# Weight products in three float32r passes, and a projected attention vector spread through DRAM, in a gated graph network kernel

## The chip, the cores and the metric

The kernel runs on one core of a Trainium2 chip. The metric is the device time of one execution in microseconds. The five engines are named as in the profile: PE is the matrix engine (PEld are its weight loads), DVE the vector engine, ACT the scalar engine, POOL the general engine, and SP the queue that issues most DMAs.

## The reference

There are 64 independent graphs of 256 nodes with 256 features each (all float32), and a 0/1 adjacency matrix of 256 x 256 for each. Two layers are applied.

```python
def layer_0(h, adj, weight, w_ih, w_hh, b_ih, b_hh):
    A = (adj != 0)
    for i in range(3):
        m = h @ weight[i]
        aggr = A.T @ m                       # per graph
        h = gru_cell(aggr, h, w_ih, w_hh, b_ih, b_hh)
    return h

def gru_cell(inp, h, ...):
    i_r, i_z, i_n = split(inp @ w_ih.T + b_ih)
    h_r, h_z, h_n = split(h @ w_hh.T + b_hh)
    r, z = sigmoid(i_r + h_r), sigmoid(i_z + h_z)
    n = tanh(i_n + r * h_n)
    return (1 - z) * n + z * h

def layer_1(x, adj, W, a):                   # graph attention
    h = x @ W.T
    e = leaky_relu((h @ a_left)[:, :, None] + (h @ a_right)[:, None, :])
    alpha = softmax(where(adj == 0, -1e9, e))
    return alpha @ h

x = x + layer_0(relu(layernorm(x)), adj, ...)
x = x + layer_1(relu(layernorm(x)), adj, W, a)
```

## The kernel before

The graphs are worked in 32 pairs. A pair of graphs gives 512 columns[...]. States are kept transposed (features on the partitions), in two blocks of 128 features.

**Setup.** The matrices that don't depend on the graphs are formed once. Since `A.T @ (h @ weight[i]) @ w_ih.T` equals `(A.T @ h) @ (weight[i] @ w_ih.T)`, the kernel forms the product G of `weight[i]` and `w_ih.T` for each of the three steps (L436 to L450). The weights come by DMA (`w load`, L363), are turned on PE by transposes (L374 and L420) and copied to SBUF by ACT (L381). A product block is 128 x 384. There are 12 of them: three steps, two halves of 768 columns, and two blocks of rows. Each takes two float32 matmuls (L446), which the trace shows as four records.

**Factors.** The large matmuls of the gates run in float32r. To keep float32 accuracy, `factor` (L392) makes three parts of each matrix: part 0 on ACT (L395), part 1 on DVE (L397) and part "d" on DVE (L400). `split` (L469) makes three such parts of each operand that comes from the graphs, on ACT (L472) and DVE (L473, L475). A gate's product (`gate`, L487) is then formed in three steps: the parts 0 and 1 ("top", L497), a scaling of the bank by ACT (L511), and the part d on top of it ("rest", L502).

**The attention vector.** The scores need `h @ a_left`, which is `x @ (W.T a_left)`. The kernel forms the two rows `W.T a` (L459 to L467). It broadcasts each column of `a` to 128 columns, so that one matmul gives the row on all 128 partitions, and copies the bank of 128 x 512 to `va` on DVE. The "dot" operations on DVE (L715) read `va`.

**The gates.** Each of three steps of a pair has `prop` (L618: the sum over neighbours), then for each of two feature blocks the gates r, nh (hidden part of n), ni (input part of n) and z. ACT does tanh for r (L637), n (L647) and z (L650), and DVE combines them (L642, L645, L654, L656, L658). `back` turns the state for the next step on PE (L685), or by DMA (L522, L527) with a copy on ACT (L535).

**Attention.** Normalisation (L550 to L563), dots (L715), leaky (L741), mask and max (L744, L746) and exp (L752) are followed by `mix` (L769), `project` (L778, or L792 for the last pairs, in float32), and the result (L797). The right-hand scores of all pairs but the last go through a row in DRAM and are spread to 128 partitions by a second DMA (L724, L727). The last pair is worked in finer pieces: its third step of gates in two halves of 256 columns ("of 0" and "of 1"), and its attention for each block of 128 rows (L807 to L838).

**What sets the order.** Nothing is issued in program order. Every operation is recorded with a duration, a latency and the buffers that it reads and writes, and a planner (`Plan.run`, L139) places them all. It takes the operation that can start first by its own estimates, and among those that can start together the one with the lowest priority value:

```python
                    if fits and (best is None or (t, o.prio, o.seq) < best[0]):
                        best = ((t, o.prio, o.seq), o)
```

The priority value comes from due times and from the latencies of what follows. A table `LEAD` (L27) shifts the priority of operations by name. Names of the first pair begin with "first", those of the last two pairs with "late" and "last"; an entry without such a word works on all pairs. The result is one fixed sequence for each engine.

Of the kernel before, what the change touches and what calls it, by code (L numbers as in the profile page):

```python
# [10 lines left out]
F32 = mybir.dt.float32  # L11
# [3 lines left out]
AF = mybir.ActivationFunctionType  # L15
ALU = mybir.AluOpType
# [8 lines left out]


LEAD = {  # L27
    "w load": 17000, "w d": -3000, "in 0 eps": -2000, "in 0 relu": 71000, "in 1 stats": -3000, "in 1 relu": 57000,
    "h0 0": 3000, "prop 0": 4000, "g0 0": -24000, "g0 1": -19000, "prop 1": 30000, "g1 1": 23000, "r 0 topT": 2000,
    "ni 0 topF": -18000, "u add 0": 1000, "z 0 topF": -114000, "z 0 rest": 11000, "z 0": 55000, "d add 0": -14000,  # L30
    "r 1 topT": -55000, "nh 1 rest": 5000, "ni 1 topF": -23000, "z 1 topF": -162000, "z 1 scale": -94000,
    "z 1": 51000, "d sub 1": -3000, "d add 1": -14000, "back copy 1": -43000, "mask 0": -6000,
    "mid 1 stats": -52000, "max 1": -19000, "c0 0": 12000, "late h0 d": -6000, "late prop 0": 13000,
    "late g0 0": -52000, "late r 0 topT": -7000, "late nh 0 topF": -29000, "late r 1 topT": -8000,
    "late ni 1 topF": -30000, "late tanh 1": -20000, "last A": 11000, "last in 0 stats": 9000,
    "last in 0 eps": 1000, "last prop 1": 19000, "last g1 0": 12000, "last r 0 topT": -5000,
    "last r 0 rest": -45000, "last nh 1 rest": -3000, "last lo 0": -88000, "last back 1": -80000,
    "last ni 0 of 0 topF": 18000, "last nh 1 of 0 rest": -5000, "last ni 1 of 0 topF": 19000,
    "last r 0 of 1 topF": -19000, "last nh 0 of 1 topF": -34000, "last ni 0 of 1 topF": -37000,
}  # L40


# [164 lines left out]
def tile_gated_gnn_then_gat(  # L207
# [39 lines left out]
    nc = tc.nc  # L247
    P = 128
    B, N, D = x.shape
    L = weight.shape[0]  # L250
    NB = N // P
    DB = D // P
    G = 2
    E3 = 3 * D
# [6 lines left out]
    const = ctx.enter_context(tc.tile_pool(name="const", bufs=1))  # L261
    psum = ctx.enter_context(tc.tile_pool(name="psum", bufs=1, space=bass.MemoryType.PSUM))
    plan = Plan(WINDOW, LEAD)
# [7 lines left out]
    dram = ctx.enter_context(tc.tile_pool(name="dram", bufs=1, space=bass.MemoryType.DRAM))  # L271
    plan.slot_class("line", [dram.tile([1, N], F32, name=f"line{i}") for i in range(4)])

    ALL = (0, 1)
    ONE = (0,)

    def parts(b):
        return b.t[:, :GN].rearrange("p (k d) -> p k d", k=2)
# [3 lines left out]
    def pe(name, n, fn, **kw):  # L282
        return plan.op(name, "PE", n, n + 220, fn, **kw)

    def act(name, n, fn, **kw):
        plan.op(name, "ACT", n, n + 170, fn, **kw)

    def dve(name, n, fn, **kw):
        plan.op(name, "DVE", n, n + 160, fn, **kw)

    def dve2(name, n, fn, **kw):
        plan.op(name, "DVE", n, n + 160, fn, port=True, **kw)
# [8 lines left out]
    MM, TR, PROP, PASS = 432, 109, 120, 232  # L301
    A512, V512, S512, VP256, C512 = 475, 605, 660, 392, 522
    LINE, SPREAD = 4600, 4600
    SPLIT = 4096.0
    C = 1.0 / SPLIT
    BELOW = 1.0 - C / 2
# [4 lines left out]
    vec = const.tile([P, 2 * DB + 2 * EB], F32, name="vec")  # L311
# [8 lines left out]
    va = const.tile([P, 2, D], F32, name="va")  # L320
# [15 lines left out]
    def setup():  # L336
# [6 lines left out]
        def load_rows():  # L343
# [7 lines left out]
           r=[(rw, ONE), ("ident", ONE)], w=[(pt, ONE)])  # L351
# [5 lines left out]
        def rows_of(src, nblk):  # L357

            view = src.rearrange("(b q) d -> q b d", q=P)
            res = []  # L360
            for r0 in range(0, nblk, 2):
                b = Buf("full")
                dma("w load", 256, lambda b=b, r0=r0: nc.sync.dma_start(parts(b), view[:, r0 : r0 + 2, :]), w=[(b, ONE)])  # L363
                res += [(b, 0), (b, 1)]
            return res

        def transposed(dst, region, blocks, whole=None):

            def go_for(c):
                pt = Buf("bank")  # L370

                def go():
                    for r, (b, k) in enumerate(blocks):
                        nc.tensor.transpose(pt.t[:, ts(r, P)], parts(b)[:, k, ts(c, P)], ident)  # L374

                n = len(blocks)
                pe("w turn", TR * n, go, r=[(b, ONE) for b, _ in blocks] + [("ident", ONE)], w=[(pt, ONE)])
                w = n * P if whole is None else whole

                def copies():  # L380
                    nc.scalar.copy(dst(c)[:, :w], pt.t[:, :w])  # L381
                    if w < n * P:
                        nc.scalar.mul(dst(c)[:, w:], pt.t[:, w : n * P], 0.5)

                act("w copy", (140 if w == n * P else 260) + n * 110, copies, r=[(pt, ONE)], w=[region(c)])

            for c in range(DB):
                go_for(c)

        H = E3 // 2  # L390

        def factor(m, b, n, dst, key, bank=True):  # L392

            src = lambda: b.t[:, :n]
            act("w 0", (100 if bank else 140) + 0.75 * n, lambda: nc.scalar.activation(dst(0), src(), AF.Copy, scale=C * BELOW),  # L395
                r=[(b, ONE)], w=[(f"fac{m}", (key + (0,),))])
            (dve if bank else dve2)("w 1", 75 + 1.04 * n, lambda: nc.vector.scalar_tensor_tensor(  # L397
                dst(1), dst(0).bitcast(F32), -SPLIT, src(), op0=ALU.mult, op1=ALU.add),
                r=[(b, ONE)], w=[(f"fac{m}", (key + (0,),))])
            dve2("w d", 75 + 1.04 * n, lambda: nc.vector.tensor_sub(dst(2), dst(1).bitcast(F32), dst(0).bitcast(F32)),  # L400
                r=[(f"fac{m}", (key + (0,),))], w=[(f"fac{m}", (key + (1,),))])

        def part_of(m, kb, half):
            return lambda j: fac[m][:, j, kb, ts(half, H)]

        def halves():
            return [[Buf("full") for _ in range(2)] for _ in range(DB)]

        def whole(T, blocks, n=E3):
            for half in range(2):  # L410
                transposed(lambda c, half=half: T[c][half].t[:, :H], lambda c, half=half: (T[c][half], ONE),
                           blocks[3 * half : 3 * half + 3], min(max(n - half * H, 0), H))

        def bank_of(blocks, c):

            pt = Buf("bank")

            def go():
                for r, (b, k) in enumerate(blocks):
                    nc.tensor.transpose(pt.t[:, ts(r, P)], parts(b)[:, k, ts(c, P)], ident)  # L420

            pe("w turn", TR * len(blocks), go, r=[(b, ONE) for b, _ in blocks] + [("ident", ONE)], w=[(pt, ONE)])
            return pt
# [7 lines left out]
        for kb in range(DB):  # L431
            factor("hh", whhT[kb], H, part_of("hh", kb, 1), (kb, 1), bank=False)
        wih_n = rows_of(w_ih, EB)
        wihT = halves()
        whole(wihT, wih_n)
        for i in range(L):  # L436
            w_n = rows_of(weight[i], DB)
            w_T = Buf("full")
            transposed(lambda c, w_T=w_T: parts(w_T)[:, c, :], lambda c, w_T=w_T: (w_T, (c,)), w_n)
            for half in range(2):  # L440
                for db in range(DB):
                    pg = Buf("bank")

                    def go(pg=pg, half=half, db=db, w_T=w_T):
                        for kb in range(DB):
                            nc.tensor.matmul(pg.t[:, :H], parts(w_T)[:, kb, ts(db, P)], wihT[kb][half].t[:, :H],  # L446
                                             start=(kb == 0), stop=(kb == DB - 1))

                    pe("G", 3 * MM, go, r=[(w_T, ALL)] + [(wihT[kb][half], ONE) for kb in range(DB)], w=[(pg, ONE)])
                    factor(i, pg, H, part_of(i, db, half), (db, half))  # L450
        W_n = rows_of(W, DB)
        Wb = W_n[0][0]
        for c in range(DB):
            w_T = bank_of(W_n, c)
            dve("w keep", 330, lambda c=c, b=w_T: nc.vector.tensor_copy(wT[:, c, :], b.t[:, :D]), r=[(w_T, ONE)], w=[("wT", (c,))])
            factor("W", w_T, D, lambda j, c=c: fac["W"][:, j, c, :], (c,))
        pl = Buf("bank")

        def go():  # L459
            for n in range(2):  # L460
                for ob in range(DB):
                    c = n * DB + ob
                    nc.tensor.matmul(pl.t[:, ts(n, D)], vec[:, c : c + 1].to_broadcast([P, P]), parts(Wb)[:, ob, :],
                                     start=(ob == 0), stop=(ob == DB - 1))

        pe("va", 4 * MM, go, r=[(Wb, ONE), ("vec", ONE)], w=[(pl, ONE)])
        dve("va copy", V512, lambda: nc.vector.tensor_copy(va, pl.t.rearrange("p (n d) -> p n d", n=2)), r=[(pl, ONE)], w=[("va", ONE)])  # L467

    def split(name, v, bank=False):  # L469

# [369 lines left out]

    TOPS, SLOT = {}, 20
    setup()
    for p in range(NPAIR):
        if p > 0:
# [31 lines left out]
```

## Time and profile before

| | |
|---|---|
| three runs | 2074.25, 2075.97 and 2076.62 us |
| span of the profiled execution | 2066.4 us |
| PE busy | 2045.3 us (99%) |
| DVE busy | 1737.0 us (84%) |
| ACT busy | 1761.8 us (85%) |
| L446, products G | 48 records of 128 x 384 |
| L497 and L502, gates | 2328 + 2328 and 1164 + 1164 matmuls |

A row of the profile's groups names the line, the engine, the operation and what it writes and reads. After a bar stand the total busy time and the mean time of one, and after a second bar the engine's idle time just before such instructions, with what ended it. The chain that ended last is followed back from the last instruction, at each step to what released it. Matmul ends are modelled and overlap the next start, so the time of a matmul is best read from the chain or from one start to the next.

### The profile page before, as it was taken

Reading aid. Unit: us, or ns where it says so; the run is one execution under the profiler, and the core shown is the slowest. Engines: PE = TensorE matmul, PEld = TensorE weight load, DVE = VectorE, ACT = ScalarE, POOL = GpSimd, SP = SyncE. Lnnn points to the kernel's source line nnn. Section 1 sums busy time; section 2 is a strip of 40 time slices with the busy share of each in tenths; the row PEclk is TensorE's granted clock in tenths of the full one; section 3 lists DMA queues with packets and bytes.
Section 4 is the critical chain, followed back from the end, with each engine's and each line's share of the span. In section 5 each row is a group of like instructions: output and inputs, shape, how many; then the busy total and the mean of one; then the engine's idle time right before and its main releaser. Section 6 shows DMA issues by size and latency. Waiting matters only on the chain.

```text
span 2066.4 us, 31380 instructions
## 1 busy us (share of the span) xinstructions
PE 2045.3 (99%) x9949; PEld 1692.7 (82%) x9949; DVE 1737.0 (84%) x3888; ACT 1761.8 (85%) x3047; POOL 157.8 (8%) x198
## 2 busy tenths in 40 slices
PE   8999999999999999999999999999999999999998
PEld 6888888888887888888888888888888888788887
DVE  7788888888888888888888888888888888888877
ACT  6788898888888888888888888888888888888876
POOL 1000000000000000000000000000000000000000
PEclk9999999999999999999999999999999999999999
DMA  4257787657776667866676766777766778666632
GB/s 129 55 108 122 128 142 108 116 106 139 132 125 104 117 121 130 141 109 113 110 136 129 125 115 117 111 133 140 112 115 118 121 128 142 104 118 108 118 72 57
DMA packets 742918, 241.52 MB, mean 117 GB/s; under 512 B 666704, under 2 KB 742752, under 8 KB 742752
## 3 DMA queue, kind: packets, MB, share of 16 engines
q1 hardware_dynamic: 742720, 239.51, 65.6%
q8 instruction: 78, 1.28, 0.3%
q14 instruction: 88, 0.72, 0.1%
q10 hardware_dynamic: 32, 0.01, 0.0%
HBM read 61.09 MB, written 16.84 MB: 38 GB/s over the span
## 4 chain that ended last, share of the span: by engine, by line
PE 85%; DMA 5%; DVE 5%; ACT 3%; issue 1%; SPq 0%; ACTq 0%; DVEq 0%
PE bank L497 45%; PE bank L502 23%; PE bank L618 8%; DMA full<-full 5%; PE bank L778 4%; PE bank L769 4%; DVE round L473 1%; ACT full L535 1%; PE bank L446 1%; DVE round L475 1%; ACT full L563 1%; ACT bank L511 1%; DVE full L656 0%; DVE full L744 0%; ACT full L637 0%
## 5 line engine op out<-in xcount | busy, mean ns | idle before, releaser
L497 PE MATMUL bank<-round,fac 128*128 128x512 f32 (+1 forms) x2328 | 617.2, 393 | 0.4
L497 PE MATMUL bank<-round,fac_hh 128*128 128x512 f32 (+1 forms) x2328 | 612.4, 395 | 0.0
L497 PEld LDWEIGHTS bank<-round,fac 128*128 128x128 f32 x2328 | 433.7, 188 | 105.3 <-DVE round L473 2.0
L497 PEld LDWEIGHTS bank<-round,fac_hh 128*128 128x128 f32 x2328 | 430.6, 188 | 96.4
L511 ACT ACTIVATE bank<-bank 128x512 f32<-128x512 f32 (+1 forms) x582 | 334.6, 577 | 95.8 <-PE bank L497 88.0
L535 ACT COPY full<-full 128x1024 uint16<-128x1024 uint16 x308 | 358.9, 1165 | 31.3 <-DMA full<-full 23.6
L502 PE MATMUL bank<-round,fac 128*128 128x512 f32 (+1 forms) x1164 | 356.8, 392 | 0.2 <-ACT bank L511 0.2
L502 PE MATMUL bank<-round,fac_hh 128*128 128x512 f32 (+1 forms) x1164 | 354.1, 394 | 0.0
L475 DVE SCALAR_TENSOR_TENSOR round<-round,round 128x512 fp32r<-128x512 f32 x444 | 304.8, 688 | 8.1
L502 PEld LDWEIGHTS bank<-round,fac 128*128 128x128 f32 x1164 | 215.1, 188 | 55.4 <-ACT bank L511 6.0
L557 POOL TENSOR_TENSOR small<-small,nhalf 128x2 f32<-128x2 f32 x128 | 123.8, 975 | 1687.2 <-DVE small L555 1611.4
L502 PEld LDWEIGHTS bank<-round,fac_hh 128*128 128x128 f32 x1164 | 206.1, 188 | 44.9 <-ACT bank L511 7.4
L618 PEld LDWEIGHTS bank<-round,round 128*128 128x128 f32 x1536 | 208.6, 190 | 14.4 <-DVE round L696 0.5
L473 DVE TENSOR_TENSOR round<-bank,round 128x512 fp32r<-128x512 f32 x252 | 172.8, 686 | 56.2 <-ACT round L472 53.3
L618 PE MATMUL bank<-round,round 128*128 128x256 f32 x1536 | 215.9, 284 | 0.3 <-DVE round L696 0.3
L642 DVE SCALAR_TENSOR_TENSOR full<-full,bank 128x512 f32<-128x512 f32 (+1 forms) x194 | 131.7, 679 | 56.4 <-ACT full L637 52.0
L647 ACT ACTIVATE full<-full,vec 128x512 f32<-128x512 f32 (+1 forms) x194 | 139.4, 719 | 40.4 <-DVE full L645 20.5
L650 ACT ACTIVATE full<-bank,b_rz 128x512 f32<-128x512 f32 (+1 forms) x194 | 132.8, 684 | 45.5 <-PE bank L502 43.9
L472 ACT ACTIVATE round<-bank 128x512 fp32r<-128x512 f32 x252 | 145.9, 592 | 28.5 <-PE bank L618 26.7
L656 DVE SCALAR_TENSOR_TENSOR full<-full,full 128x512 f32<-128x512 f32 (+1 forms) x194 | 130.4, 672 | 32.3 <-ACT full L650 32.1
L473 DVE TENSOR_TENSOR round<-full,round 128x512 fp32r<-128x512 f32 x192 | 130.9, 682 | 27.5 <-ACT round L472 24.2
L645 DVE TENSOR_TENSOR full<-full,bank 128x512 f32<-128x512 f32 (+1 forms) x194 | 131.1, 676 | 24.4 <-PE bank L502 17.4
(98 smaller groups left out, 2292.8 us busy)
## 6 DMA issues: line engine op xcount, KB each, us to landing
full<-full SPq DMA_DIRECT2D x492, 128.0 KB, 3.6
x<-in_x_dram SPq DMA_DIRECT2D x64, 256.0 KB, 3.0
adj<-in_adj_dram SPq DMA_DIRECT2D x64, 256.0 KB, 4.3
full<-in_x_dram SPq DMA_DIRECT2D x64, 256.0 KB, 3.1
full<-full SPq DMA_DIRECT2D x248, 64.0 KB, 2.5
out_dram<-full SPq DMA_DIRECT2D x62, 256.0 KB, 2.5
full<-line SPq DMA_DIRECT2D x62, 128.0 KB, 3.7
full<-full SPq DMA_TRANSPOSE x308, 3.2
```

Source lines behind the costliest of these rows:

```text
L472: act(name + " 0", A512 if bank else C512, lambda: nc.scalar.activation(v0.t, v.t, AF.Copy, scale=BELOW), r=[(v, ALL)], w=[(v0, ONE)])
L473: (dve if bank else dve2)(name + " 1", V512, lambda: nc.vector.tensor_sub(v1.t, v.t, v0.t.bitcast(F32)), r=[(v, ALL), (v0, ONE)], w=[(v1, ...
L475: dve2(name + " d", V512, lambda: nc.vector.scalar_tensor_tensor(vd.t, v1.t.bitcast(F32), -SPLIT, v0.t.bitcast(F32), op0=ALU.mult, op1=ALU ...
L497: nc.tensor.matmul(bank.t[:, cols], f(m, j, kb), b.t[:, cols], start=(first and n == 0), stop=True, skip_group_check=True)
L502: nc.tensor.matmul(bank.t[:, cols], f(m, 2, kb), s[kb][2].t[:, cols], start=False, stop=True, skip_group_check=True)
L511: act(name + " scale", fit(575 if "nh" in name else 515, part), lambda: nc.scalar.activation(bank.t[:, cols], bank.t[:, cols], AF.Identity ...
L535: act(name, 1065, lambda: nc.scalar.copy(dst.t.bitcast(U16).rearrange("p (j n b) -> p j n b", j=2, b=2), src.t.bitcast(U16).rearrange(f"p ...
L618: nc.tensor.matmul(pa.t[:, ts(g, N)], b, parts(A[g])[:, sb, :], start=(n == 0), stop=(n == len(terms) - 1))
L642: dve(f"u {db}{of}", fit(S512, part), lambda u=u, k=ph, b=r_, cols=cols: nc.vector.scalar_tensor_tensor(u.t[:, cols], b.t[:, cols], 1.0, k ...
L645: dve(f"u add {db}{of}", fit(V512, part), lambda u=u, k=pn, cols=cols: nc.vector.tensor_add(u.t[:, cols], u.t[:, cols], k.t[:, cols]), r=[ ...
L647: act(f"tanh {db}{of}", fit(615, part), lambda u=u, en=en, cols=cols: nc.scalar.activation(u.t[:, cols], u.t[:, cols], AF.Tanh, bias=b_i[: ...
L650: act(f"z {db}{of}", fit(575, part), lambda b=z_, k=pz, db=db, cols=cols: nc.scalar.activation(b.t[:, cols], k.t[:, cols], AF.Tanh, bias=b ...
```

## The change

The products G are formed like the gates. The transposed blocks of `w_ih` and of `weight[i]` are no longer copied as they are: ACT and DVE make three float32r parts of each, straight from the bank ("wih 0", "wih 1", "wih d", "wi 0", "wi 1", "wi d"). Each product block then takes four matmuls with the parts 0 and 1 ("G top"), a scaling on ACT ("G scale") and two matmuls with the parts d ("G rest"). The factors of G are made from the bank as before.

The rows `W.T a` are formed as two rows on two partitions: the two columns of `a` are the stationary operand, and two matmuls take the place of four. DVE copies the rows to a tile `two`, a DMA writes them to a row in DRAM, and a second DMA spreads that to `va` on 128 partitions.

The table `LEAD` is another one: 25 of its 56 entries stay, "w d" is changed from -3000 to -33000, "first prop 0" is new, and the others go, among them all those for the last two pairs.

```diff
 LEAD = {
...
-    "mid 1 stats": -52000, "max 1": -19000, "c0 0": 12000, "late h0 d": -6000, "late prop 0": 13000,
-    "late g0 0": -52000, "late r 0 topT": -7000, "late nh 0 topF": -29000, "late r 1 topT": -8000,
-    "late ni 1 topF": -30000, "late tanh 1": -20000, "last A": 11000, "last in 0 stats": 9000,
-    "last in 0 eps": 1000, "last prop 1": 19000, "last g1 0": 12000, "last r 0 topT": -5000,
-    "last r 0 rest": -45000, "last nh 1 rest": -3000, "last lo 0": -88000, "last back 1": -80000,
-    "last ni 0 of 0 topF": 18000, "last nh 1 of 0 rest": -5000, "last ni 1 of 0 topF": 19000,
-    "last r 0 of 1 topF": -19000, "last nh 0 of 1 topF": -34000, "last ni 0 of 1 topF": -37000,
+    "w d": -33000, "first prop 0": -4000, "in 0 relu": 71000, "in 1 relu": 57000, "prop 0": 4000, "g0 0": -24000,
...
-        wihT = halves()
-        whole(wihT, wih_n)
+        vs = {}
+        for half in range(2):
+            for kb in range(DB):
+                b = bank_of(wih_n[3 * half : 3 * half + 3], kb)
+                v0, v1, vd = vs[kb, half] = [Buf("round") for _ in range(3)]
+                act("wih 0", 390, lambda b=b, v0=v0: nc.scalar.activation(v0.t[:, :H], b.t[:, :H], AF.Copy, scale=BELOW),
+                    r=[(b, ONE)], w=[(v0, ONE)])
+                dve("wih 1", 470, lambda b=b, v0=v0, v1=v1: nc.vector.tensor_sub(v1.t[:, :H], b.t[:, :H], v0.t[:, :H].bitcast(F32)),
+                    r=[(b, ONE), (v0, ONE)], w=[(v1, ONE)])
+                dve2("wih d", 470, lambda v0=v0, v1=v1, vd=vd: nc.vector.scalar_tensor_tensor(
+                    vd.t[:, :H], v1.t[:, :H].bitcast(F32), -SPLIT, v0.t[:, :H].bitcast(F32), op0=ALU.mult, op1=ALU.add),
+                    r=[(v0, ONE), (v1, ONE)], w=[(vd, ONE)])
...
-                        for kb in range(DB):
-                            nc.tensor.matmul(pg.t[:, :H], parts(w_T)[:, kb, ts(db, P)], wihT[kb][half].t[:, :H],
-                                             start=(kb == 0), stop=(kb == DB - 1))
...
+                    def go(js, first, pg=pg, half=half, db=db, ws=ws):
+                        for n, (kb, j) in enumerate((kb, j) for kb in range(DB) for j in js):
+                            nc.tensor.matmul(pg.t[:, :H], parts(ws[j])[:, kb, ts(db, P)], vs[kb, half][j].t[:, :H],
+                                             start=(first and n == 0), stop=True, skip_group_check=True)
+
+                    pe("G top", 4 * 176, lambda go=go: go((0, 1), True),
...
+                    act("G scale", 400, lambda pg=pg: nc.scalar.activation(pg.t[:, :H], pg.t[:, :H], AF.Copy, scale=SPLIT + 1.0), w=[(pg, ONE)])
+                    pe("G rest", 2 * 176, lambda go=go: go((2,), False), r=[(ws[2], ALL)] + [(vs[kb, half][2], ONE) for kb in range(DB)], w=[(pg, ONE)])
...
+            for ob in range(DB):
+                nc.tensor.matmul(pl.t[:2, :D], vec[:, ob : 2 * DB : DB], parts(Wb)[:, ob, :], start=(ob == 0), stop=(ob == DB - 1))
...
+        dve("va copy", 335, lambda: nc.vector.tensor_copy(two.t, pl.t[:2, :D]), r=[(pl, ONE)], w=[(two, ONE)])
+        va_line = dram.tile([2, D], F32, name="va_line")
+        plan.op("va line", "SP", 450, LINE, lambda: nc.sync.dma_start(va_line, two.t), r=[(two, ONE)], w=[("va_line", ONE)])
+        plan.op("va spread", "SP", 450, SPREAD, lambda: nc.sync.dma_start(
+            va, va_line.rearrange("n d -> (n d)").rearrange("(o m) -> o m", o=1).to_broadcast([P, 2 * D]).rearrange("p (n d) -> p n d", n=2)),
+            r=[("va_line", ONE)], w=[("va", ONE)])
```

## The prediction

> **What bounds the kernel now.** I read the page first: its busy shares and the chain that ended last.
>
> ```profile
> span 2066.4 us, 31380 instructions
> ...
> PE 2045.3 (99%) x9949; PEld 1692.7 (82%) x9949; DVE 1737.0 (84%) x3888; ACT 1761.8 (85%) x3047; POOL 157.8 (8%) x198
> ...
> PE 85%; DMA 5%; DVE 5%; ACT 3%; issue 1%; SPq 0%; ACTq 0%; DVEq 0%
> ```
>
> PE is busy all but 21 us of the span. Only two things can move the time: PE work taken away, or PE idle time added or removed. Next, the stretches of 20 us place the idle time: 4.7 us before 20, 2.8 us between 40 and 60, some 4 us in all between 60 and 2000, and 9.5 us from 2000 on. The setup, which the diff rewrites, is done by 41 us; its stretch shows DVE nearly as full as PE:
>
> ```profile
> 20.00:40.00 20.00, 20.00 (x92) 14.79 (x91) 19.10 (x45) 11.60 (x23) 2.38 (x4) 1.00 0.14 45
> ```
>
> (columns: length, then busy of PE, PE loads, DVE, ACT, POOL). The chain in order of time prices the work that goes; columns are start, length, what:
>
> ```profile
> 13.20 2.58 PE bank L446 x8
> ...
> 16.21 1.73 PE bank L463 x8
> ...
> 46.40 0.95 PE bank L502 x4
> ...
> 52.59 0.98 PE bank L618 x6
> ```
>
> Eight records of a G product (L446) take 2.58 us, 0.3225 each; PE carries the chain from 4.67 to 47.36, where layer 0 of pair 0 ends, then DVE carries it to 52.59. The same view at the end:
>
> ```profile
> 2017.92 1.38 DVE full L715 x8
> ...
> 2021.67 3.45 PE bank L618 x16
> ...
> 2044.08 4.12 DMA full<-full
> ...
> 2061.37 1.74 PE bank L831 x8
> ```
>
> After 2015.84 the last pair is almost alone, and each of its dependent chains is seen. Sixteen L618 matmuls take 3.45 us there; elsewhere x8 takes 0.95. The reason is the granted clock (length, PE busy, clock, DMA):
>
> ```profile
> 2024.00:2026.00 2.00, 2.00 (x12) 0.50 0.63 62
> ```
>
> Last, the PE timeline of the end: all gate matmuls are done at 2043.9, and the second batch's softmax transposes (L815) start at 2058.5.
>
> ```profile
> 2043.37 0.50 PE L502 MATMUL bank<-round,fac 128*128 128x256 f32 x2 [0.22 <-ACT bank L511]
> ...
> 2058.47 0.60 PE L815 MATMUL bank<-ident,full 128*128 128x128 f32 x4
> ```
>
> [...]the nearest row, the line and spread DMAs of L724/L727, lands in 2.7 to 5.2 us, and I use that.
>
> **The change part by part.** *PE.* Removed: 48 L446 records, 48 x 0.3225 = 15.5 us. Added: 12 blocks x 6 matmuls of 128x384 in float32r. No such row exists; 128x256 takes 0.119 (0.95/8), 128x512 takes 0.233 (0.93/4), so 0.176 between them: 72 x 0.176 = 12.7. The va row loses half its records: 1.73 to 0.86. Transposes stay. Net -3.7 us.
>
> *DVE.* From one start to the next, two 384-wide operations take 0.94 us (16.95 to 17.89), two 256-wide 0.66 (37.74 to 38.40): 0.47 and 0.33 each. Added: 8 of 384 for w_ih (3.76), 12 of 256 for the W_i (3.96); the va copy falls from 0.60 to 0.33. Net +7.4 us, in a setup where DVE had 19.1 of 20 busy. *ACT.* Twelve G scale at 0.49: +5.9 us; ACT was 11.6 of 20, so its load is hidden, though scale is one more link between a block's products and its factors.
>
> *Setup walked through.* I laid the changed order of PE, DVE and ACT side by side with these prices. The new order loads x before the weights: DVE starts its real work at 5.1 rather than 8.5 us. First G product 9.5; second-half products 15.6; r 0 of the hidden state 17.8; the transposes of the last w_hh and W_i blocks wait for banks that DVE and ACT must empty, 19.5 to 22.5; nh 0 at 24; the eight later products 25.9 to 38; layer 0's last matmul at 47.45, against 47.36. PE gives its 3.7 us away in waits of 0.3 to 1.5 us. Then DVE, still full of the factors of layers 1 and 2, ends the state update (L658) at 50.2 against 51.3, but waits for the copies of pair 1 behind it; when the same matmuls are done, PE stands at 56.9 against 57.3. I book 0, with bounds of -3.7 (all PE work saved shows) and +3.5 (the walk with every DVE duration at its displayed length, 0.55 for 0.47, plus semaphore gaps).
>
> *va through DRAM.* The line DMA waits for the va copy at about 8.6 us; the last weight load and the loads of pair 1 queue behind it on SP. The spread waits for the line's landing (2.7 to 5.2); only adj loads of pair 2 are behind it. va is first read at 134.3 us (L715). Hidden: 0; below nothing is excluded as no PE wait in the page names these loads.
>
> *Middle.* For pairs 2 to 27 the PE order is the same; per pair 5 of 100 DVE operations change places. PE is full there: 0, within 1.
>
> *End.* The priority table loses all its "late" and "last" entries, and pairs 30 and 31 are ordered anew. First, layer 1 to 2 of pair 31: z 1 topF is now followed at once by its own rest, which must wait for the scale between (0.58 plus two handovers of 0.03): +0.6. On ACT two relu of the pair before (0.5 each) stand ahead of tanh z 1, and on DVE all eight dots (0.345 each, two of them waiting for relu behind z 1) stand ahead of d mul 1: PE takes up continuous work 6.6 us after the last matmul of the layer; before it was 5.6 (2015.84 to 2021.4): +1.0. Half clock follows in both. Sum +1.6.
>
> Second, the final layer. Let S be the start of "r 0 of 0 topF" (2028.8 before; the span ends at S+37.6). Before, all gates come first, done at S+15, and mix and project of pair 30 (L769, L792: 3.45 and 3.5 us) fill PE while the last softmax proceeds. Now mix and project stand *ahead* of ni 1, z 0 and z 1 rest of half 1. Walking PE: 13.6 at the start of mix, 20.6 at its end, z 1 rest done at S+21.8. From there: tanh z and tanh 1 0.95, d sub, d mul 0.7, two more DVE steps 0.7, mask 0, res and max 0 1.6, statistics 0.9, eps, power, shift 1.2, the copies of batch 0 and two relu to 28.95, dots to 29.65, batch 0's second project to 31.4, transpose L736 0.25, leaky 0.9, mask and max 1.35, exp 0.7: L815 at S+34.7. Before it was S+29.7. The rest (7.9 us) is the same. +5.1, with bounds of +1 (ACT and DVE overlap more than I walked) and +8.
>
> Sum: 0 + 0 + 1.6 + 5.1 = +6.7 on the span of 2066.4, so 2073.1. The three unprofiled runs lie at 2074.25 to 2076.62; the difference goes on their median: 2075.97 + 6.7 = 2082.7.
>
> **Rivals.** *The setup stays PE-bound (faster).* DVE's earlier start (3.4 us) and its waits (L642 alone waited 3.9 us in the first 60) absorb the 7.4 us, so all of 3.7 shows, and the state update comes 1.1 earlier: -4.8, 2071.2. It decides only if the end costs under 0.6 us, since 0.2% is 4.15 us. For it: PE carries the chain through the setup. Against: 19.1 of 20.
>
> *The end is cheap (same).* PE order at the end matters little because idle engines catch up: end +2, setup 0: 2078. Against it: the 14.6 us between 2043.9 and 2058.5 are one dependent chain.
>
> *DVE becomes the setup's bound (slower still).* The long walk of +3.5, [...]and the end as forecast: +10, 2086.
>
> *Not what it says.* The issue order shows top, scale, rest per block and half the va matmuls, so the edit is there; but if a float32r matmul of 384 cost as much as one of 512, the saving would be 15.5 - 16.8 + 0.9, about nothing lost or won in a setup that waits anyway.
>
> **How the numbers follow.** 0.2% of 2075.97 is about what a measurement here can tell from no change, so the borders are 2071.8 and 2080.1. Forecast 0.47; DVE-bound setup 0.20; cheap end 0.20; PE-bound setup 0.13. The likeliest gives 2082.7, its own range 2079 to 2087. Leaving out the faster case and the upper part of the DVE case gives 2073 to 2090. Faster 0.13, same 0.20, slower 0.67.
>
> **What would show it.** Right: PE busy falls by about 3.7 us while its idle time before 60 us grows by as much; z 1 rest directly after z 1 topF with a wait on ACT near the end; last gates after L792's counterpart, and 5 us more from S to the end. Wrong: PE idle in the last 60 us no longer than before, or layer 0 of pair 0 ending at 44 (PE-bound) or past 50 (DVE-bound).

## The result, and the profile after

The changed kernel takes 2084.51 us (median of 4 runs, 2083.74 to 2084.98), the kernel before 2075.11 us beside it (4 runs, 2068.92 to 2076.62): a ratio of 1.0051, 95% interval 1.0030 to 1.0072. Measured again later, beside new runs of before, it was 1.0037 (1.0023 to 1.0051). It is slower, by 0.4 to 0.5%.

The two profiled spans, 2066.4 and 2083.2 us, lie 16.8 us apart, more than the 9.4 us between the medians: the profiled execution of before was shorter than every timed run beside it. Every stage is therefore compared below over stretches that start and end at the same work.

The page of the changed kernel, first its busy shares, then the chain's shares:

```profile
span 2083.2 us, 31530 instructions
...
PE 2051.2 (98%) x9969; PEld 1697.7 (81%) x9969; DVE 1740.6 (84%) x3908; ACT 1760.2 (84%) x3059; POOL 158.8 (8%) x198
...
PE 83%; DMA 6%; DVE 6%; ACT 4%; issue 1%; SPq 0%; ACTq 0%; DVEq 0%
```

PE's busy time has *risen* by 5.9 us, though PE work was taken out. Counted over the same work, it fell by 2.3 us up to pair 0's first mix, rose by 3.8 from there to the first mix of pair 29, and rose by 4.4 from there to the end. The rise in the middle is scatter between executions (see "Both kernels once more"). At the end the same work takes longer at a lower clock, 0.50 in parts of it, as is shown below.

In the first 60 us PE was busy for 12.53 + 19.30 + 16.94 = 48.77 us against 52.56, that is -3.8. But the changed kernel had also done less by then. Up to the same matmul (59.04 us here, 57.33 before) it is 47.81 against 49.89: -2.1. The stretch that was quoted of before, now (length, PE, PE loads, DVE, ACT, POOL, clock, DMA):

```profile
20.00:40.00 20.00, 19.30 (x101) 16.66 (x100) 19.55 (x51) 14.50 (x35) 2.38 (x4) 1.00 0.10 28
```

and the records in the chain of waits that answer to those of before (start, length):

```profile
7.21 1.11 PE bank L405 x4
8.33 1.79 PE bank L467 x4
...
34.30 2.79 PE bank L449 x16
...
47.60 0.95 PE bank L513 x4
...
54.28 1.93 PE bank L629 x14
```

Sixteen float32r products of 384 columns take 2.79 us, 0.174 each. Four va records at the kernel's start take as long as eight did before (1.79 us against 1.73). PE works slowly in the first microseconds: the four transposes (L405) ahead of va take 1.11 us, 0.28 each, where sixteen in before, from 11.45 on, took 1.75, 0.11 each. The profile has no clock below 1.00 there, so the cause stays open. Layer 0 of pair 0 ends at 48.55 (47.36 before). In this profile DVE, not PE, carries the chain from 11.05 to 25.82.

At the end, the timeline of PE (start, length, line, tiles, count, and in brackets the idle time before it with what ended it):

```profile
2050.39 3.62 PE L780 MATMUL bank<-full,full 128*128 128x256 f32 x16
2053.85 3.62 PE L803 MATMUL bank<-wT,full 128*128 128x256 f32 x16
...
2058.25 0.40 PE L513 MATMUL bank<-round,fac 128*128 128x256 f32 x2
...
2061.30 0.44 PE L681 MATMUL bank<-ident,full 128*128 128x128 f32 x2 [1.20 <-DVE full L669]
2063.49 1.18 PE L826 MATMUL bank<-ident,full 128*128 128x128 f32 x4 [1.76 <-ACT full L818]
2064.70 3.78 PE L834 MATMUL bank<-full,full 128*128 128x128 f32 x16
2068.28 2.04 PE L842 MATMUL bank<-wT,full 128*128 128x256 f32 x8
2070.15 0.38 PE L747 MATMUL bank<-ident,small 128*128 128x128 f32 x2
2073.57 0.93 PE L826 MATMUL bank<-ident,full 128*128 128x128 f32 x4 [3.05 <-ACT full L818]
2074.47 2.98 PE L834 MATMUL bank<-full,full 128*128 128x128 f32 x16
2077.24 2.66 PE L842 MATMUL bank<-wT,full 128*128 128x256 f32 x8
```

Mix and project of pair 30 (L780, L803) stand as one block of 6.9 us ahead of the last gates (L513), as forecast. In before, the same work stood in pieces, with a back transpose (L670) between mix (L769) and project (L792), and the closing mixes (L823) took 2.05 us:

```profile
2044.44 1.99 PE L769 MATMUL bank<-full,full 128*128 128x256 f32 x8 [0.57 <-ACT full L535]
2046.27 0.69 PE L670 MATMUL bank<-ident,full 128*128 128x128 f32 x4
2047.17 1.99 PE L792 MATMUL bank<-wT,full 128*128 128x256 f32 x8 [0.20 <-ACT full L788]
...
2054.86 2.05 PE L823 MATMUL bank<-full,full 128*128 128x128 f32 x16
```

After the block the PE waits lengthen, and the closing mixes (L834) take 3.78 and 2.98 us. The stretches of after give the reason (length, PE, clock, DMA):

```profile
2060.00:2062.00 2.00, 0.53 (x3) 0.93 0.11 36
...
2066.00:2068.00 2.00, 2.00 (x11) 0.50 0.00 0
...
2076.00:2078.00 2.00, 2.00 (x9) 0.50 0.00 0
```

Before, the clock was 1.00 from 2028 to the end.

**The ruler for the end.** From the start of the last pair of 512-wide gate matmuls in pair 31's layer 1 (its second step; 2015.18 before, 2023.35 after) to the end of the span, all kernels do the same work, but for the idle matmuls that e8b adds. That stretch hardly scatters, as the table shows, while whole runs scatter by some 10 us. It is 51.3 us before and 59.8 us after: +8.6.

### The profile page after: what moved, and what is told of

It reads as the page before. It is cut to its first block, busy times and chain, and to the rows that moved or that the text cites. A ratio compares the mean times of both kernels' runs of the same rounds, so it can differ in the third digit from the quotient of the medians.

```text
span 2083.2 us, 31530 instructions
## 1 busy us (share of the span) xinstructions
PE 2051.2 (98%) x9969; PEld 1697.7 (81%) x9969; DVE 1740.6 (84%) x3908; ACT 1760.2 (84%) x3059; POOL 158.8 (8%) x198
## 4 chain that ended last, share of the span: by engine, by line
PE 83%; DMA 6%; DVE 6%; ACT 4%; issue 1%; SPq 0%; ACTq 0%; DVEq 0%
PE bank L508 44%; PE bank L513 22%; PE bank L629 7%; DMA full<-full 5%; PE bank L789 4%; PE bank L780 4%; DVE round L484 1%; ACT full L546 1%; DVE round L486 1%; ACT full L574 1%; ACT bank L522 1%; DVE full L755 1%; DVE small L757 0%; DVE full L667 0%; PE bank L449 0%
## 5 line engine op out<-in xcount | busy, mean ns | idle before, releaser
L513 PE MATMUL bank<-round,fac 128*128 128x512 f32 (+1 forms) x1164 | 357.4, 392 | 0.0
L513 PE MATMUL bank<-round,fac_hh 128*128 128x512 f32 (+1 forms) x1164 | 354.5, 394 | 1.0 <-ACT bank L522 1.0
L513 PEld LDWEIGHTS bank<-round,fac 128*128 128x128 f32 x1164 | 215.0, 188 | 55.5 <-ACT bank L522 6.1
L513 PEld LDWEIGHTS bank<-round,fac_hh 128*128 128x128 f32 x1164 | 205.9, 188 | 45.7 <-ACT bank L522 8.6
L483 ACT ACTIVATE round<-bank 128x512 fp32r<-128x512 f32 x252 | 146.0, 592 | 31.4 <-PE bank L629 30.2
L707 DVE TENSOR_TENSOR round<-full,round 128x512 fp32r<-128x512 f32 x122 | 83.9, 688 | 72.2 <-ACT round L706 72.2
```

The source lines that it names most:

```text
L483: act(name + " 0", A512 if bank else C512, lambda: nc.scalar.activation(v0.t, v.t, AF.Copy, scale=BELOW), r=[(v, ALL)], w=[(v0, ONE)])
L513: nc.tensor.matmul(bank.t[:, cols], f(m, 2, kb), s[kb][2].t[:, cols], start=False, stop=True, skip_group_check=True)
```

## The experiments

Theory A: the end loses the time, because the priority table lost its "late" and "last" entries. Rival B: the setup loses it (more work on DVE and ACT, one more link per product). Rival C: the setup stays bound by PE and gains 3.7 us. Each ratio is to runs of the kernel before on the same chip, with its 95% interval; the column before the last has the start of pair 0's first mix, in us.

| kernel | setup | table at the end | ratio (interval) | pair 0's mix at | end stretch |
|---|---|---|---|---|---|
| before | old | old | 1 | 165.2 | 51.3 |
| before, second profile | old | old | 1.0000 (0.9990 to 1.0011) | 165.6 | 50.4 |
| e3: va alone | old, new va | old | 0.9982 (0.9976 to 0.9989) | 165.4 | 50.2 |
| e3 repeated | old, new va | old | 0.9990 (0.9984 to 0.9996) | 163.6 | 49.9 |
| e2: products alone | new products | old | 1.0009 (1.0003 to 1.0016) | 166.7 | 50.5 |
| e5: after + end entries | new | old | 1.0004 (0.9996 to 1.0012) | 169.3 | 50.5 |
| e4: after + whole old table | new, old entries | old | 1.0049 (1.0036 to 1.0062) | 174.1 | 50.5 |
| e6: before - end entries | old | new | 1.0046 (1.0030 to 1.0062) | 166.8 | 60.2 |
| after | new | new | 1.0051 (1.0030 to 1.0072) | 167.0 | 59.8 |
| after, second profile | new | new | 1.0037 (1.0023 to 1.0051) | 168.2 | 59.7 |
| e7: block later | new | new, mix later | 1.0056 (1.0042 to 1.0070) | 169.2 | 59.5 |
| e8b: fillers | new | new | 1.0038 (1.0023 to 1.0052) | 166.2 | 55.9 |
| e9: block spread | new | new, tail fixed | 1.0018 (1.0011 to 1.0026) | 167.0 | 52.7 |

**The end entries, given back to after (e5) and taken from before (e6).** Each edit is in the table alone:

```
e5, on after:   LEAD += {"late h0 d": -6000, ... "last ni 0 of 1 topF": -37000}   (all "late" and "last" entries)
e6, on before:  LEAD -= the same entries
```

The order at the end is then exactly before's in e5 and exactly after's in e6; each keeps its own setup.

> The changed kernel with the late and last entries of the old table put back; its setup is the changed one's, its issue order over the end the one of before. Theory A (the end costs the time): the stretch from the start of r 0 of 0 topF to the end falls from 46.0 us back to about 37.6, the setup stays 1.7 us behind, so about 2075 + 2 = 2077 us. Rival B (the setup and its passes cost the time): it stays at about 2084 us.

> The kernel before with only the late and last entries of its table taken out; its setup is its own, its issue order over the end the changed kernel's. Theory A: the end alone costs 1.2 + 8.4 us, so about 2084 us. Rival B: about 2075 us, as before.

The two end stretches change sides with the entries: 50.5 us for e5, 60.2 us for e6. So do the times: 1.0004 and 1.0046. The entries alone, in a kernel whose setup is untouched, cost 0.46% of the 0.51%. Theory A holds.

**The parts of the setup, each alone (e2, e3).**

```
e2, on before:  whole(wihT, wih_n), w_T, "G"  ->  vs, ws, "G top", "G scale", "G rest"   (va and table as before)
e3, on before:  "va" 4 records, "va copy" 512 wide  ->  "va" 2 rows, "va line", "va spread"
```

> The kernel before with the G products in three float32r passes; va as before, the old table. Theory A: the end's order is the old one, and PE loses in waits what it saves in passes: within 3 us of before, 2073 to 2078 us. Rival B: about 2084 us. Rival C (PE-bound setup): the 3.7 us of saved passes show, about 2071 us.

> The kernel before with va formed as two rows and spread through DRAM, products and table as before. Theory A: va is first read at 134 us, so the two DMAs are hidden and 0.9 us of PE work goes: -0.9 to 0 us. Rival (the two waiting DMAs hold back the loads of pairs 1 and 2 on SP): PE waits in the first 110 us, +2 us or more.

The products alone cost 0.09%: rival C's gain of 3.7 us is refuted, and what is left of rival B is some 2 us. The two-row va was expected to bring 0.9 us at most and brought 0.10 to 0.18%, 2.4 to 4.0 us in two measurements. Both its DMAs are hidden (spread issued at 14.2 us in the changed kernel, landed 4.3 us later, first read beyond 130). Pair 0's mix comes at 165.4 and 163.6 against 165.2 and 165.6; an earlier setup explains at most a part. Where the rest of e3's gain lies stays open. It is the fastest kernel measured here.

**The whole old table on after (e4).**

```
e4, on after:  LEAD = the table of before, all of it
```

> The changed kernel's products and its two-row W^T a, under the whole table of entries of the kernel before. If the parts add up, the new products (+2.1 us alone) and the two rows (-4.0 us alone) give 2071 to 2073 us, a little faster than before, and the whole loss lies in the table. If the gain of the two rows came from where it put the setup and the new products undo it, 2074 to 2077. If the old entries don't fit the new setup, 2078 or more.

Of the expected cases only the last fits: 1.0049, with an end as short as before's (50.5). The loss sits in the setup. Its stretch (length, PE, clock, DMA) and its longest PE waits from 20 to 60 us (line waited for, total, times, longest):

```profile
20.00:40.00 20.00, 17.43 (x92) 1.00 0.10 28
```

```profile
PE bank L515 <- DVE round L491: 2.8, 1, 2.8
PE bank L703 <- DVE full L676: 1.2, 1, 1.2
PE bank L515 <- DVE fac L397: 1.1, 1, 1.1
```

PE waits for DVE, and behind these waits the clock stands at 0.50 from 57.6 to 64.4 us. Pair 0's mix comes at 174.1, 5 to 8 us later than in the profiles with the new setup entries (166.2 to 169.3). Rival B's mechanism is thus real, and the new table keeps it small. Eight entries differ between e4 and e5; which of them does it (`"w d": -33000` and `"first prop 0"` are the new values, six others are gone) was not tested one by one. The two halves of the table edit have opposite signs: in the new code the setup half gains about 0.45% (e4 against e5, 4.8 us of it at pair 0's mix), and the missing end half costs as much. The old code under the new setup entries was not run.

**What in the end costs: block or gates? (e7)**

```
e7, on after:  LEAD += {"late mix 0": -60000, "late mix 1": -60000}
```

> The changed kernel with two entries added to its table that put off the two mixes of pair 30 (and with them their projects) until the last gate matmul of pair 31 is issued; nothing else of the order of TensorE moves. Theory A (pair 30's mix and project ahead of the last gates: the gates end 7 us later, then the last pair has nothing to fill its waits): the end gets back most of what it lost, 5 to 8 us, so 2077 to 2080 us, and the clock stays full in the last 20 us. Rival A2 (what costs is the order of the gates themselves, tops and rests, which was also tuned by the entries that were taken out): the time stays within 2 us of the changed kernel's 2084.5.

The remedy that I had drawn from theory A falls here. PE's timeline in e7:

```profile
2046.90 0.40 PE L514 MATMUL bank<-round,fac 128*128 128x256 f32 x2
2047.14 3.62 PE L781 MATMUL bank<-full,full 128*128 128x256 f32 x16
2050.60 3.62 PE L804 MATMUL bank<-wT,full 128*128 128x256 f32 x16
2054.05 0.60 PE L682 MATMUL bank<-ident,full 128*128 128x128 f32 x4
...
2059.32 1.17 PE L827 MATMUL bank<-ident,full 128*128 128x128 f32 x4 [3.05 <-ACT full L819]
```

The gates now come first, and the end stretch is 59.5 us: nothing that shows is won. The block merely moved from in front of the gates to in front of the two last back transposes (L682), which are the next link of the same chain. They run at 2054.05, 7 us after the last gate. The half clock is back as well: the closing mixes (L835) take 3.78 and 3.36 us, against 2.05 in before, and the mean granted clock of the run is 0.994.

**The block spread (e9).** Setup, gates and all earlier work keep after's order; only the tail of PE's order is fixed, to one like that of before:

```
e9, on after:  every "last ... of 1 rest" before "late mix 0", then in this order:
  "late mix 0", "last back 0 of 1", "last back 1 of 1", "late project 0", "last right 0", "late mix 1",
  "late project 1", "last p turn 0 0", "last p turn 0 1", "last right 1", "last mix 0 0"
```

> The changed kernel with the tail of TensorE's order fixed to one like that of the kernel before: the two mixes of pair 30 and their projects no longer stand as one block of 7 us but one by one behind the last gates (mix 0, the two last backs, project 0, first right, mix 1, project 1, the p turns of the first graph, second right, its mixes). Setup, gates and everything earlier keep the changed kernel's order. The run that only put the block behind the gates won nothing: its last gate ended 7 us earlier and its end came as late. Theory A' (the block costs wherever it stands ahead of a link of the last pair's chain, and right 1 costs behind the mixes): the last gate ends 14.4 us after the first top of the last layer, as there, and the end follows 22.5 to 25 us later, as in before, so the end takes 37 to 39.5 us and not 46, the clock stays full, and the ratio to before is 1.000 to 1.002. Rival A2 (the order of the gates is what costs): 1.004 or more.

```profile
2051.53 0.44 PE L691 MATMUL bank<-ident,full 128*128 128x128 f32 x2 [0.56 <-DVE full L679]
...
2053.09 1.89 PE L813 MATMUL bank<-wT,full 128*128 128x256 f32 x8
...
2061.83 0.38 PE L757 MATMUL bank<-ident,small 128*128 128x128 f32 x2
...
2066.76 2.05 PE L844 MATMUL bank<-full,full 128*128 128x128 f32 x16 [0.24 <-ACT full L839]
```

The back transposes (L691) go ahead of the projects (L813), the second right (L757) ahead of the first graph's mixes, and the end stretch falls to 52.7 us: 7.1 of the 8.6 us are back, 1.0018. The gates keep their order among themselves and the setup is the same, so the cause is the order of this tail: the block ahead of links of the last chain, and the second right behind the mixes. The order of the gates (rival A2) is not what costs. The run moves both at once and doesn't price them apart. No moment of the last 20 us is below full clock (1.00 from 2064 to 2072, and L844's mixes take 2.05 us), so the gain has the half clock in it.

**The price of the half clock (e8b).**

```
e8b, on after:  k transposes of ident into a spare bank, behind
                "last right 0": 5, "last back 0 of 1": 8, "last back 1 of 1": 12, "last right 1": 22
```

> The changed kernel with idle transposes of the identity into a bank of their own in four places where TensorE waits near the end: 5 behind the first right, 8 and 12 behind the last two backs, 22 behind the second right, some 0.12 us each at full clock, a little short of each wait. All other order is the changed kernel's. It prices the half clock: in the changed kernel the last p turns, mixes and projects took 4.5 us more than at full clock. Theory A1 (that half clock follows from the waits just before it): the clock stays at 1.00 in the last 20 us and the time falls by 3 to 5 us, a ratio to before of 1.003. Rival (the clock falls for another reason, or the waits alone are the loss): no gain, 1.005 to 1.007, since the fillers then run at half clock and lie ahead of the p turns.

The order is after's, with idle matmuls in PE's waits (L283):

```profile
2062.04 0.38 PE L758 MATMUL bank<-ident,small 128*128 128x128 f32 x2
2062.26 2.56 PE L283 MATMUL bank<-ident 128*128 128x128 f32 x22
2065.50 0.93 PE L838 MATMUL bank<-ident,full 128*128 128x128 f32 x4 [0.67 <-ACT full L830]
2066.40 2.05 PE L846 MATMUL bank<-full,full 128*128 128x128 f32 x16
```

The mixes take 2.05 us again, the clock is 1.00 from 2060 until the last matmul, and the end stretch is 55.9 us, 3.9 us shorter than after's. Of that, 0.6 lies ahead of the first filler, where the clock came back a little earlier than in after: the sixteen matmuls of prop take 2.68 us there, against 3.23. From S on (the start of "r 0 of 0 topF", as in the prediction; 2030.8 here, 2037.2 in after) the end takes 42.7 us and not 46.0. The fillers are thus worth 3.3 us, within the expected 3 to 5. The whole run's ratio of 1.0038 can't be told from the 1.0037 and 1.0051 of after; the stretch can. With the tail spread (e9) the end takes 39.2 us from S, and 37.6 in before. So of the 8.4 us that the change adds from S on, 3.3 are half clock, 3.5 more go with the order of the tail, and 1.6 are not placed.

**Both kernels once more.**

> The kernel before once more, unchanged, for a second profile and for the scatter of its own runs. Every theory expects a ratio of 1.000 with an interval of about 0.001 on either side. What is asked of it is the middle: the profile shown so far was the shortest of its runs. If the 5 us by which the changed kernel falls behind between pair 0 and pair 30 in the two profiles are scatter between executions, this profile shows the first mix of pair 30 later than the first profile did by 2 to 9 us, at the same order of instructions. If they are a cost of the change, it shows it at the same place within 1 us.

> The changed kernel itself once more, since its ratio came from four runs and the later experiments were timed on other chips than it. Theory A' and all rivals: 1.004 to 1.006 again, so that the 1.0018 with the tail spread and the 1.0038 with the fillers can be set against it. Below 1.004 the tail's share would be smaller than told so far.

> The kernel before with only the two-row W^T a, the same file as before, which was 0.18% faster than before though its setup reached the first mix no earlier. If that gain belongs to the kernel: 0.9976 to 0.9989 again. If it was that chip's or that hour's: 0.9995 to 1.0005. Its profile is wanted too: pair by pair, the first mix of pair 30 against 1822 to 1824 us after that of pair 0 in the two profiles of before.

Between the first mixes of pairs 0 and 29 (the mix that those texts count as pair 30's) before takes 1823.6 and 1822.3 us, after 1828.6 and 1824.3. Before's second profile was not later, as I had thought possible; the scatter shows in other kernels. The seven profiles under the old order of the middle lie at 1822.3 to 1831.8, mean 1826.1; the six under the new one at 1822.6 to 1828.6, mean 1825.4. The 5 us in the first pair of profiles are scatter; the middle costs nothing that shows.

Pair 0's mix scatters too, and here the scatter goes with the clock. Under the new setup the mix comes at 166.2 and 167.0 us where the clock stays full (e8b, after), at 167.0 where it stands at 0.50 for 3.4 us between 51 and 61 us (e9), and at 168.2 to 169.3 where it does so for 6.8 us (after's second profile, e5, e7).

## Why the prediction was right

The side, and the place of the main loss, were right: +6.7 us forecast on the median, 9.4 and 8.2 measured. That the number came so near was in part luck: in the profiles the end, booked at +6.7, came to 1.2 + 8.4 = +9.6, and the setup, booked at 0, to nearly +2.

*Setup, booked at 0.* The price of a product was right, 0.174 us against 0.176. The saving of 3.7 us on PE was not: over the same work PE is busy 2.1 us less. One term of it was wrong in kind: va was to save 0.87 us, but its four records took 1.79 at the slow pace of the start. That DVE's additions eat the saving was right. Layer 0 ends at 48.55 against 47.45 forecast, and the same matmuls are done at 59.04 against 57.33 before: +1.7, inside the bounds. Pair 0's mix averages 167.8 over six profiles of this setup against 165.9 over three of the old one.

*va DMAs and middle, 0 each.* Right.

*Transition of pair 31 from layer 1 to 2 (its second step to its third), +1.6.* Counted from the end of "r 1 rest", it is +1.2. The stall was seen as forecast, 0.67 us of waiting for ACT ahead of "z 1 rest".

*Final layer, +5.1.* This is the term that was mis-sized: S is 2037.17 after, and the span ends at S+46.0, against S+37.6: +8.4. The walk was near until the last gate (21.3 against 21.8 forecast) and is near for the whole order once the clock is full, as e8b shows: "right 1" at S+31.3 (forecast 31.4), the second p turns at S+34.7 (34.7), the end at S+42.7 (42.6). The half clock is what was missed, in two places:

- In after, the first graph's mixes take 3.78 us, so "right 1", which the order puts behind its projects (the walk had it so), runs at S+33.0 instead of 31.4, and the second p turns at S+36.4: +1.7.
- "The rest (7.9 us) is the same" is the step that failed: it took 9.6 us, much of it at half clock (0.50 from 2075.39 to 2078.80); +1.7.

5.1 + 1.7 + 1.7 = 8.5, against 8.4 measured. I had booked half clock at the transition, where it came (0.50 in after from 2027.61, within a PE wait of 4.33 us, to 2034.42), and not behind the waits that I myself was adding. The waits ahead of the fall at 2061.73 were shorter, 0.79 and 1.20 us (see the last section). In before the 0.50 ran from 2019.46 to 2026.29, behind 3.41 us in which PE had worked for 0.66.

That mix and project ahead of the last gates delay the end was right for this order. What does not follow is that moving them behind the gates would mend it: e7 wins nothing. Before's mix and project lay *between* the links of the last chain and filled its waits.

*The rivals.* PE-bound setup: refuted by e2. DVE-bound setup: not in this kernel, but e4 shows it, at +8.9 us on pair 0's mix, once the new setup entries are taken away; and half clock in the setup is there in some executions (0.50 for 6.8 us in after's second profile, e5 and e7), at some 2 us on that mix. Cheap end: refuted by e6. "Not what it says": refuted by the 0.174 us.

## What to carry to other kernels

When the last tiles drain, one dependent chain sets the end, and bulk work on its engine should be cut to fit the chain's waits. Here a block of 6.9 us ahead of a link cost about as much in front of the gates as in front of the back transposes. The longer waits on TensorE were paid twice here, in the wait and in the half clock behind it (3.3 us of the 8.4, by e8b), so a walk through the waits of an order needs the granted clock in it. When an edit also replaces tuned priorities, cross the two (new code under old table, old code under new table), since their parts can cancel: here the setup entries gained what the missing end entries lost.

## What the hardware showed that I had not expected

- In after the clock also fell to half without a single long wait. From 2058.87 PE was given two pairs of transposes, after waits of 0.79 and 1.20 us, and at 2061.73 the granted clock fell to 0.50: sparse work did not hold it.
- In these thirteen profiles each stretch at half clock that the span's end doesn't cut lasts 3.4 or 6.8 us (in before 6.83, in after 6.81, 6.82 and 3.41). In the 3.41 us (the shortest of these) before a fall PE was busy for 0.66 us in before, and for 0, 1.42 and 1.76 us in after (falls at 2027.61, 2061.73 and 2075.39); in the 3.41 us before each of these four returns to 1.00 it was busy for all of them. Little work was not always followed by a fall: between 2070.00 and 2073.41 in after PE was busy for 0.53 us, and the clock stayed at 1.00 until 2075.39.
- A fall came after the work had resumed. The wait of 3.05 us in after ended at 2073.57; the two microseconds from 2074 were granted 0.85, the next 0.50.
- Idle transposes of the identity in the waits, in one of them 22 in 2.56 us (0.116 each), were enough to keep full clock through the same waits (1.00 from 2060 to 2068 in e8b).
- Whole runs of one kernel scatter by about 10 us (before: 2068.99 to 2078.91 in 51 runs), while the end stretch of one order repeats within 0.1 us (59.8 and 59.7) to 0.9 us (51.3 and 50.4). The 0.9 is the half clock ahead of S, 6.8 us long in one profile and 3.4 in the other; from S on, these two ends are 37.6 us both. A stretch between two marks of the same work measured 3.3 us that the run time could not.
